# Layer 1's values in couples: seven block products beside keys and queries, values kept in DRAM

## The chip, the core and the metric

The kernel runs on one core of a Trainium2 chip. Everything is float32. The metric is the device time of one execution in microseconds (us); a measurement is the median of several runs.

A core has five engines that run their own queues in order: PE (matrix products; weights are loaded by an instruction of their own, PEld), DVE (elementwise and reductions), ACT (copies and functions such as the exponential), POOL (used here for a few additions) and SP, which here only issues DMAs. Products land in banks of PSUM, 128 partitions by 512 numbers; ACT or DVE take them from there to SBUF. DRAM is reached by DMA alone.

## The reference

Two layers on an input of 2 batches, 512 channels and 64x32 = 2048 tokens. The change touches the second one's attention, a Nystrom attention with 8 heads of 64 and 256 landmarks.

```python
# layer 0: softmax attention over 2048 tokens, with a residual; then
def _L1_attn_ref(x, Wqkv, Wout, bout, conv_w):        # x: layer-normalised tokens
    qkv = x @ Wqkv
    q, k, v = jnp.split(qkv, 3, axis=-1)
    q, k, v = (tohead(q), tohead(k), tohead(v))
    q = q * scale
    qL = q.reshape(b, h, m, l, d).sum(axis=3) / l     # landmarks: means of l = 8 tokens
    kL = k.reshape(b, h, m, l, d).sum(axis=3) / l
    attn1 = softmax(einsum('bhid,bhjd->bhij', q, kL))
    attn2 = softmax(einsum('bhid,bhjd->bhij', qL, kL))
    attn3 = softmax(einsum('bhid,bhjd->bhij', qL, k))
    attn2_pinv = moore_penrose_iter_pinv(attn2, 6)    # six iterations of 256x256 products
    out = attn1 @ (attn2_pinv @ (attn3 @ v))
    res = conv_general_dilated(v, conv_w, ...)        # 33 taps along the tokens, per head
    return (out + res).transpose(0, 2, 1, 3).reshape(b, n, h * d) @ Wout + bout

t = t + _L1_attn_ref(_ln_t(t), ...)
t = t + _L1_ffn_ref(_ln_t(t), ...)                    # one 512x512 map
```

## The kernel before

Heads go in pairs: a pair is 2 heads, 128 columns of a weight. There are 4 pairs in each of 2 batches. Tokens go in 4 blocks (`TB` = 512), the 512 channels in 4 chunks of 128 (`KC`). A 1 MB tile holds 128 rows by 2048 tokens, or 512 channels by 512 tokens.

The order of work on PE, DVE, ACT and POOL is the order in which the program is written: generators yield after a few instructions, and others are advanced between. DMAs on SP may be placed earlier than they are written, when what they wait for is done.

**Keys and queries of layer 1** (`Unit`, `products`, `others`; about 1366 to 1653 us). For a pair, the key and query weights (512x256) against two blocks of tokens (512x1024) are two by two blocks, and seven products of blocks replace eight (Winograd's form of Strassen's scheme). Sums of weights come from `Pair.combine_w` (4 additions on DVE), differences of tokens from `Combined.sums` (4 for each half of the tokens, made once for all pairs). A unit is one pair with one half of the tokens. Its products 1, 6, 7 and 4 are chained: they accumulate in one bank, which ACT copies out after each; products 2, 5 and 3 go to two other banks and are added to the copies by DVE. In the order of issue products 4 and 3 of a unit stand inside the next one: 1, 4 of the last, 2, 3 of the last, 6, 5, 7. `between` and `meanwhile` start loads of the next pair's weights, and attention 2 of the pair before: scores and exponentials (`attend`), then the Gram matrix (`gram`). `later` and `last_of_all` are lists of small DVE calls (landmark sums, largest entries for a bounds check); `some()` makes one of them. `stored` sends finished keys and queries to DRAM. Pair 0 of the first batch is done earlier, beside layer 0's attention; `ORDER` weaves the others of that batch with the rest of layer 0.

**Values** (`values`, `values_of_tokens`, L1148 to L1160). A pair's values are computed with a weight of their own (`prefetch_w`) by plain products: for each block of tokens 4 parts by 4 chunks, each 128x128 by 128 columns; ACT copies the bank out. The result stays in SBUF. The first pair's values stand in the products' stage (`START`), the second's before the iterations, the others' among the last steps of the pair two places earlier (`vals`). For the first batch's pairs, which come second, the tokens are loaded again (`xh2`).

**The iterations** (`pinv`, from 1672 us, one pair after the other: the second batch's pairs, then the first's). Five iterations, each with the squares `pa` and `pb` for two heads, then the last steps: three rounds of a product `wp`, its copy by ACT, transposes `tp`, and a subtraction by DVE, each needing the one before. `chunk(c)` puts other work behind iteration c: for c = 0 to 3 a part of attention 3 of the next pair (`sc<-L,k`, `av<-p,v`) and a block of attention 1 of the pair before (`sc<-q,L`, `av<-p,u`, row sums `rs`, and 1/sums, which eight DMAs from `spread` copy over partitions, `rinv`); for c = 4 the row sums of attention 3 and the convolution of the next pair, four banks in one go (`convolution`, L1781). `last(i)` with i = 0 to 5 puts work between the last steps: values, the next pair's landmark work (`landmarks_values`, `start_values`), and the next attention's first scores. `n_ones` is the number of blocks of attention 1 in the chunks: four, in the last two pairs three and the fourth in `last`. From the fifth pair on, `TURNS` says where units of the second batch's finish (`f`: output projection, norm, map) are made; `o` are units of its last block made early. `TAIL` orders what is left after the last pair. Convolutions wait in SBUF; two of them (`o_d`) in DRAM. Keys and values share a ring of two 1 MB buffers (tag "v").

Of the kernel before, what the change touches and what calls it, by code (L numbers as in the profile page):

```python
# [16 lines left out]
P = 128  # L17
B, C, H, W = 2, 512, 64, 32
S = H * W
# [18 lines left out]
def general_path(  # L38
# [623 lines left out]
TURNS = (  # L662
    (",,,", "f,,,", "f,,,", "f,,,", "f,", "f,f,f,f,f,"),
    ("f,,,", "ff,,,", "f,,,", "f,,,", "f,", "f,f,f,f,f,f"),
    ("fff,,,", "ff,,,", "f,,,", "f,,,", "ff,", ",f,f,f,f,"),
    ("fffoo,,,", "f,f,f,", "f,f,f,", "ff,,oo,", "f,", ",f,,f,f,ff"),
)

TAIL = "11fffnf11f1ff1afafff1f1f1f1faas11bsbs11bbt"
# [4 lines left out]
START = "v....v...,a,v,,,0,1,v".split(",")  # L674

PREFETCH = 26
# [12 lines left out]
def fast_path(  # L689
# [54 lines left out]
    k_d = dram.tile([B, NPAIR, P, S], F32, name="k_fd")  # L744
    X_d = dram.tile([B, NPAIR, 2, P, 2, LM], F32, name="X_fd")
# [728 lines left out]
    class Pair:  # L1474
# [14 lines left out]
        def begin(self, *kinds):  # L1489
            self.w = getattr(self, "w", {})  # L1490
            for j in kinds or (1, 0):
                self.w[j] = self.load_w(j)

        def keys_and_queries(self, pool, tag, xhs, k=None):

            self.begin_landmarks(NTB)
            if k is None:
                k = kvpool.tile([P, S], F32, tag="k", name=f"k_{self.name}")
            q = pool.tile([P, S], F32, tag=tag, name=f"q_{self.name}")
            for t in range(NTB):  # L1500
                toks = slice(t * TB, (t + 1) * TB)
                for j, dst in ((1, k), (0, q)):
                    pp = bank(f"pp{j}_{self.name}_{t}")
                    for c in range(KC):
                        nc.tensor.matmul(
                            pp, lhsT=self.w[j][:, c, :], rhs=xhs[t][:, c, :], start=c == 0, stop=c == KC - 1
                        )
                    nc.scalar.copy(dst[:, toks], pp)
                    for call in self.stored(j, t, dst[:, toks], toks):
                        call()  # L1510
                    yield
            self.bounds()
# [74 lines left out]
        def two(self, kind, name):  # L1587

            name = f"{name}_{self.i}"
            if self.b == 0 and self.hp + 1 < NPAIR:  # L1590
                p = ppool.tile([P, 4 * (LM + 1)], F32, tag="p", name=name)
                p = p.rearrange("p (h k n) -> p h k n", h=2, k=2)
                return [p[:, h] for h in range(2)]
            return [zpool.tile([P, 2, LM + 1], F32, tag=f"{kind}{h}", name=f"{name}_{h}") for h in range(2)]
# [66 lines left out]
        def prefetch_w(self, w=None):  # L1661
            self.w2 = self.load_w(2, w)

        def prefetch(self):
# [3 lines left out]
            nc.sync.dma_start(self.L[0], L_d[self.b, self.hp][:, 0, :])  # L1668
            self.band = lmpool.tile([P, 2, BAND], F32, tag="band", name=f"band_{self.name}", bufs=1)
# [3 lines left out]

        def values(self, xhs):
            v = kvpool.tile([P, NST, P], F32, tag="v", name=f"v_{self.name}")
            self.v = v
            for t in range(NTB):
                values_of_tokens(v, t, xhs[t], lambda k: self.w2[:, k, :], self.name)
                yield
# [101 lines left out]
        def convolution(self, o):  # L1781

            self.o = o
            for t in range(NTB):
# [22 lines left out]
                if t % 2:  # L1807
                    yield
# [147 lines left out]
        def attn1_end(self, t):  # L1956

            rinv, toks = self.rinv1, slice(t * TB, (t + 1) * TB)
            nc.vector.tensor_tensor(rinv, self.av1[t], rinv, ALU.mult)  # L1959
            nc.gpsimd.tensor_tensor(self.o[:, toks], self.o[:, toks], rinv, ALU.add)  # L1960

# [226 lines left out]
    class Unit:  # L2188

        def __init__(self, pair, tp, part):
            self.pair, self.tp, self.part = pair, tp, part
            self.name = f"{pair.name}_{tp}"

        def begin(self, banks_of):
            if self.pair.b == 0 and (self.pair.hp, self.tp) in ((2, 0), (3, 1)):
                d = kvpool.tile([P, NST, P], F32, tag="v", name=f"kq_{self.name}").rearrange("p a b -> p (a b)")
            else:
                d = kvpool.tile([P, S], F32, tag="k", name=f"kq_{self.name}")  # L2200
# [3 lines left out]
        def product(self, to, m, start=True):  # L2204
            w, x = self.pair.ws[m], self.part.of[m]
            for k in range(2):
                nc.tensor.matmul(  # L2207
                    to, lhsT=w[:, k, :], rhs=x[:, k, :], start=start and k == 0, stop=k == 1, skip_group_check=True
                )
# [35 lines left out]
    def products(units, banks_of, between, meanwhile):  # L2245
# [25 lines left out]
        for n, u in enumerate(units):  # L2271
            if n > 2 - u.pair.b:
                until(lambda: not units[n - 3 + u.pair.b].left)
            if u.tp == 0:
                u.pair.begin_landmarks(2)
            u.begin(banks_of)
# [28 lines left out]
        yield  # L2305
        third(last)
        yield

    def others(b, first, parts, banks_of, after=lambda tp: None):

        units = [Unit(pair, tp, part) for pair in pairs[b][first:] for tp, part in enumerate(parts)]
        fronts = {}

        def begin(hp):
            pairs[b][hp].begin()
            fronts[hp] = pairs[b][hp].combine_w()

        def meanwhile(u, m):

            hp = u.pair.hp  # L2320
            if m == 2 and u.tp == 1 and hp:
                before = pairs[b][hp - 1]
                until(lambda: all(before.marked))
                later[:0] = before.attend()
                yield
            if m == 7 and u.tp == 1 and hp:
                until(lambda: pairs[b][hp - 1].attended)
                for h in range(2):
                    pairs[b][hp - 1].gram(h)
                    yield  # L2330

        def between(u, m):
            hp = u.pair.hp
            if m == 2 and u.tp == 1:
                if hp + 1 < NPAIR:
                    begin(hp + 1)
                elif b + 1 < B:
                    pairs[b + 1][0].begin()
            if m == 7 and u.tp == 1 and hp + 1 < NPAIR:
                later.extend(fronts[hp + 1][:3])  # L2340
            if m == 3 and hp + 1 == NPAIR and u.tp == 1:
                after(0)
            if m == 3 and u.tp == 0 and hp > first:
                later.append(fronts[hp][3])

        yield from products(units, banks_of, between, meanwhile)
# [5 lines left out]
    def load_next(tp):  # L2352
        assert over
        next_xhs.extend(load_x(xh_d, 1, "xh", 2 * tp, 2))
# [14 lines left out]
    pairs[0][1].begin()  # L2369
    later.extend(pairs[0][1].combine_w())  # L2370
    later.extend(parts[1].sums())
    more = [others(0, 1, parts, banks_first, load_next)]
# [48 lines left out]
    over = True  # L2421
    while more:
# [8 lines left out]
    xhs = next_xhs  # L2431
    def beside_second(x1lo):
        flat = [qopool.tile([P, S], F32, tag="qo", name=f"t{j}_second") for j in range(2)]
        return [t[:, lo : lo + 2 * TB].rearrange("p (k n) -> p k n", k=2) for t in flat for lo in (0, 2 * TB)]

    parts = [Combined(*xhs[2 * tp : 2 * tp + 2], beside_second) for tp in range(2)]
    todo = pairs[1] + pairs[0]

    def values(n):

        yield from todo[n].values(xhs_of[n // NPAIR])
        if n == NPAIR - 1:
            xhs_of.append(load_x(xh_d, 0, "xh2"))

    def convolution(n):

        name = f"o_{todo[n].name}"
        if n <= NPAIR:
            o = qopool.tile([P, S], F32, tag="qo", name=name)
        else:  # L2450
            o = None if n < len(todo) - 1 else late_buffer(name)
        return todo[n].convolution(o)

    def second_of_first():
# [3 lines left out]
        for part in (landmarks, conv, landmarks, start, conv):  # L2458
# [9 lines left out]


    xhs_of = [xhs]  # L2470
    todo[0].prefetch_w(block_of(lpool, "xr", "w2_first")[:, :, :P])
    later.extend(parts[0].sums())
    later.extend(todo[0].combine_w())
    later.extend(parts[1].sums())
    firsts = [values(0)]

    def beside(events):
        for c in events:
            if c == "v":
                advance(firsts)  # L2480
            elif c == "a":
                until(lambda: all(pairs[0][-1].marked))
                later[:0] = pairs[0][-1].attend()
            elif c in "01":
                until(lambda: pairs[0][-1].attended)
                pairs[0][-1].gram(int(c))
            else:
                some()

    beside(START[0])  # L2490
    first = second_of_first()
    for i, _ in enumerate(others(1, 0, parts, banks_second)):
# [6 lines left out]
        if i + 1 < len(START):  # L2499
            beside(START[i + 1])  # L2500
        if i == PREFETCH:
            todo[0].prefetch()
        if i >= PREFETCH + 6 and i % 2:
            next(first, None)
    for _ in first:
        some(2)
    todo[1].prefetch_w()


# [4 lines left out]
    vals = [values(1)]  # L2514
    advance(vals)
    until(lambda: all(todo[NPAIR - 1].marked))
    later[:0] = todo[NPAIR - 1].attend()
    advance(vals)
# [291 lines left out]
```

## Time and profile before

| what | us |
|---|---|
| median of 3 runs (2649.33 to 2650.98) | 2649.54 |
| the profiled execution | 2649.55 |
| its span | 2647.7 |
| PE busy in 0 to 1240 (layer 0, mostly) | 1233.08 of 1240.00 |
| PE busy in 1240 to 1366 | 125.55 of 126.00 |
| PE busy in 1672 to 1755 (the first pair's iterations) | 83.00 of 83.00 |
| PE busy in 1851 to 2377 (pairs three to seven) | 523.92 of 526.00 |
| PE busy in 2474 to 2647 (the tail) | 164.02 of 173.00 |

The span is what the profiler saw of the program. A group's row of the page holds line, engine, operation, written<-read tiles, shapes and count, then busy time, mean of one in ns, and the engine's idle time ahead of them with what ended it. A row of the timeline holds start, length, engine, line, operation and tiles; a row of waits between brackets names the instruction that ended the wait. A matmul's length includes its way through the array, so rows overlap: what one costs is read from start to start.

### The profile page before, as it was taken

To read this page: it belongs to the slowest core of one execution; us is meant where nothing else is said; L and a number is where in the kernel's file an instruction comes from. 1 tells how busy PE (TensorE), PEld (TensorE's weight loads), DVE (VectorE), ACT (ScalarE), POOL (GpSimd) and SP (SyncE) were. 2 spreads that over 40 slices of the span, in tenths; PEclk is the share of its full clock that TensorE was granted. 3 is DMA by queue.
4 is the path that set the end of the run, shared out by engine and by line. 5 is a ranking of instruction groups with operands and counts; after the bars stand their busy time and mean duration, and the time that the engine had idled before them with its cause. 6 is when DMAs were issued, how large, how long until landed. Compare 5 with 4: busy or idle time off the path is not lost.

```text
span 2647.7 us, 41440 instructions
## 1 busy us (share of the span) xinstructions
PE 2623.1 (99%) x16882; PEld 1353.3 (51%) x16882; DVE 1780.1 (67%) x2259; ACT 921.0 (35%) x1398; POOL 169.6 (6%) x127
## 2 busy tenths in 40 slices
PE   9999999999999999999999999999999999999998
PEld 5343443444344344353344555777677666665444
DVE  5788897886667778767867866544644645465665
ACT  1444453443344434435522323223333232231310
POOL 0011011000001100000002000000000000000000
PEclk9999999999999999999999999999999999999999
DMA  4011011201221201011115633213111112121211
GB/s 147 22 30 36 13 33 49 77 21 52 88 80 58 91 25 32 25 56 60 41 44 182 225 125 118 98 33 129 48 37 61 60 45 100 34 81 36 97 35 49
DMA packets 123608, 177.16 MB, mean 67 GB/s; under 512 B 16784, under 2 KB 77968, under 8 KB 120848
## 3 DMA queue, kind: packets, MB, share of 16 engines
q1 hardware_dynamic: 117264, 153.15, 17.8%
q0 software_dynamic: 5440, 20.97, 2.0%
q8 instruction: 134, 2.20, 0.4%
q14 instruction: 66, 0.54, 0.1%
q10 hardware_dynamic: 704, 0.31, 0.0%
HBM read 94.02 MB, written 63.57 MB: 60 GB/s over the span
## 4 chain that ended last, share of the span: by engine, by line
PE 91%; DVE 6%; issue 1%; ACT 1%; DMA 1%; SPq 0%; DVEq 0%; ACTq 0%
PE av_f L1319 15%; PE sc_f L1289 15%; PE pb L1866 5%; PE pa L1866 5%; PE vp_f L1153 4%; PE yp_g L1168 4%; PE yp_f L1168 4%; PE fp_g L2022 4%; PE vp L1153 4%; PE pc_f L1021 3%; PE pu L2207 3%; DVE acc_f L1307 3%; PE pu_f L1021 2%; PE sc L1695 2%; PE sc L1923 2%; PE av L1716 2%
## 5 line engine op out<-in xcount | busy, mean ns | idle before, releaser
L1297 ACT ACTIVATE p_f<-sc_f 128x1024 f32<-128x1024 f32 x512 | 496.5, 1021 | 540.2 <-PE sc_f L1289 540.0
L1307 DVE TENSOR_TENSOR acc_f<-acc_f,p_f 128x1024 f32<-128x1024 f32 x448 | 575.3, 1284 | 110.8 <-ACT p_f L1297 83.9
L1319 PE MATMUL av_f<-p_f,v_f 64*64 64x512 f32 x4096 | 494.4, 589 | 2.8 <-DVE q_f L1326 2.8
L1289 PE MATMUL sc_f<-q_f,k_f 64*64 64x512 f32 x4096 | 489.9, 591 | 0.3 <-ACT p_f L1297 0.3
L1319 PEld LDWEIGHTS av_f<-p_f,v_f 64*64 64x64 f32 x4096 | 162.5, 133 | 286.8 <-issue 274.3
L1289 PEld LDWEIGHTS sc_f<-q_f,k_f 64*64 64x64 f32 x4096 | 154.2, 133 | 282.2 <-issue 277.2
L1866 PE MATMUL pa<-M 128*128 128x192 f32 (+1 forms) x640 | 150.3, 380 | 0.0
L1866 PE MATMUL pb<-R 128*128 128x192 f32 (+1 forms) x640 | 149.3, 380 | 0.6 <-DVE M L1879 0.6
L1153 PEld LDWEIGHTS vp_f<-wv_f,x 128*128 128x128 f32 x1024 | 115.8, 192 | 5.5 <-issue 5.2
L1866 PEld LDWEIGHTS pb<-R 128*128 128x128 f32 x640 | 106.5, 190 | 23.6 <-DVE M L1879 0.8
L1866 PEld LDWEIGHTS pa<-M 128*128 128x128 f32 x640 | 108.2, 193 | 19.8 <-ACT M L1857 2.0
L1153 PE MATMUL vp_f<-wv_f,x 128*128 128x128 f32 x1024 | 117.9, 276 | 0.0
L1168 PE MATMUL yp_g<-o,wo_f 128*128 128x512 f32 x256 | 113.8, 595 | 0.0
L1168 PE MATMUL yp_f<-q_f,wo_f 128*128 128x512 f32 x256 | 112.4, 595 | 0.1
L1339 POOL TENSOR_TENSOR q_f<-q_f,rinv_f 128x512 f32<-128x512 f32 x32 | 49.0, 1530 | 970.1 <-DMA rinv_f<-acc_f 647.5
L1153 PE MATMUL vp<-w,xh 128*128 128x128 f32 x896 | 105.8, 276 | 0.0
L1153 PEld LDWEIGHTS vp<-w,xh 128*128 128x128 f32 x896 | 102.2, 192 | 5.4 <-issue 3.5
L1879 DVE SCALAR_TENSOR_TENSOR M<-M,pb 128x320 f32<-128x320 f32 (+1 forms) x160 | 60.1, 417 | 60.8 <-PE pb L1866 60.8
L2022 PE MATMUL fp_g<-xn_g,mT 128*128 128x512 f32 (+1 forms) x232 | 99.3, 579 | 0.0
L1928 ACT ACTIVATE p<-sc 128x512 f32<-128x512 f32 x128 | 66.7, 602 | 91.6 <-PE sc L1923 91.1
L1960 POOL TENSOR_TENSOR o<-o,rinv 128x512 f32<-128x512 f32 x32 | 44.4, 1386 | 772.9 <-DVE rinv L1959 587.5
L1879 DVE SCALAR_TENSOR_TENSOR R<-M,pa 128x320 f32<-128x320 f32 (+1 forms) x160 | 58.5, 407 | 42.1 <-PE pa L1866 42.1
(293 smaller groups left out, 3215.9 us busy)
## 6 DMA issues: line engine op xcount, KB each, us to landing
xh<-xh_fd SPq DMA_DIRECT2D x12, 1024.0 KB, 7.9
rinv_f<-acc_f SPq DMA_DIRECT2D x256, 32.0 KB, 1.9
xr_f<-in_x_dram SPq DMA_DIRECT2D x8, 1024.0 KB, 5.2
x_fd<-xr_f POOLq DMA_DIRECT2D x8, 1024.0 KB, 4.7
xh_fd<-xn_f POOLq DMA_DIRECT2D x8, 1024.0 KB, 4.4
k_fd<-kq SPq DMA_DIRECT2D x16, 512.0 KB, 2.6
q_fd<-kq SPq DMA_DIRECT2D x16, 512.0 KB, 3.2
k<-k_fd SPq DMA_DIRECT2D x8, 1024.0 KB, 6.0
```

Of the source, the lines that this page charges most:

```text
L1021: nc.tensor.matmul(to, lhsT=w[:, k, :], rhs=x[:, k, :], start=start and k == 0, stop=k == 1, skip_group_check=True,)
L1153: nc.tensor.matmul(vp[:, j * P : (j + 1) * P], lhsT=xb[:, k, j * P : (j + 1) * P], rhs=w_of(k), start=k == 0, stop=k == KC - 1,)
L1168: nc.tensor.matmul(yp, lhsT=wo_sb[:, k, m * P : (m + 1) * P], rhs=oTs[k][:, toks], start=k == 0, stop=k == NPAIR - 1,)
L1289: nc.tensor.matmul(sc[r * D : (r + 1) * D, h, :], lhsT=hd.k[rows, lo : lo + D], rhs=hd.q[rows, t * TB : (t + 1) * TB], start=True, stop=True,)
L1297: nc.scalar.activation(p, sc, AF.Exp, scale=D**-0.5)
L1307: nc.vector.tensor_tensor(acc, first if c == 1 else acc, p, ALU.add)
L1319: nc.tensor.matmul(av[r][half, :], lhsT=hd.v[keys, c, half], rhs=pp[keys, h, :], start=c == 0, stop=c == NST - 1,)
L1866: nc.tensor.matmul(dst, lhsT=lhsT[:, k, t * P : (t + 1) * P], rhs=rhs[:, k, :], start=k == 0, stop=k == 1)
L1879: nc.vector.scalar_tensor_tensor(out, m, scale, pr, ALU.mult, ALU.subtract)
L1928: nc.scalar.activation(p[:, h, :], sc, AF.Exp, scale=D**-0.5)
L2022: nc.tensor.matmul(fp[:, cols], lhsT=mT[:, k, m * P : (m + 1) * P], rhs=self.xn[:, k, cols], start=k == 0, stop=k == KC - 1,)
L2207: nc.tensor.matmul(to, lhsT=w[:, k, :], rhs=x[:, k, :], start=start and k == 0, stop=k == 1, skip_group_check=True)
```

## The change

The values of two pairs of one batch become a `Couple`, which stands in the products' stage like a pair: its two weights take the place of key and query weights, and its two halves of tokens are two `Unit`s of seven products. As values are needed with tokens on partitions, tokens are now the left operand: `operands` splits a product of 512 columns into four parts of 128 columns. `ITEMS` gives the order for a batch (4 and 5 are the couples of pairs 0, 1 and 2, 3). Values go to DRAM (`v_d`) and come back by `prefetch_v`, a pair ahead; keys come by `prefetch_k` from the last steps of the pair before that. The plain products of layer 1's values, their weights' loads, the second load of the first batch's tokens and the way of two convolutions through DRAM go.

The convolution yields after each block, and `LAST` puts its four portions (c), the rest of the landmark work (l) and the start values (s) between the last steps. Attention 1 has three blocks in the chunks and the fourth in the last steps for every pair that has one before it. The first batch's four couple-halves run after `ORDER` is through; the second batch's tokens are loaded in two steps, the first already there. With the second batch's last couple stand attention 2 of its last pair and the start of the iterations (`at_end`); in the table `at`, True stands for the scores of the pair before and False for its Gram products, and a pair gives its unit and product. `TURNS`, `OUTS` and `TAIL` place units of the finish anew.

```diff
+TURNS = "000020000200110001001111|300010000000111020100020|310010001000100000221110|310020002000200010011222"
+OUTS = "000001000000001001000000"
+LAST = "c|lc|s|c|cs|"
+ITEMS = "12345", "041235"
-TAIL = "11fffnf11f1ff1afafff1f1f1f1faas11bsbs11bbt"
+TAIL = "11fffnf11f1ff1afafff1f1faf11fas11bsbs11bbt"
-START = "v....v...,a,v,,,0,1,v".split(",")
-PREFETCH = 26
+PREFETCH = 36
...
+    v_d = dram.tile([B, NPAIR, P, S], F32, name="v_fd")
...
+        def operands(self, w, x):
+            return [(slice(0, TB), [(w[:, k, :], x[:, k, :]) for k in range(2)])]
...
-        def prefetch(self):
+        def prefetch_k(self):
             self.k = kvpool.tile([P, S], F32, tag="v", name=f"k2_{self.name}")
             nc.sync.dma_start(self.k, k_d[self.b, self.hp])
...
+        def prefetch_v(self):
+            self.v = kvpool.tile([P, NST, P], F32, tag="v", name=f"v_{self.name}")
+            nc.sync.dma_start(self.v, v_d[self.b, self.hp].rearrange("p (c d) -> p c d", d=P))
...
-                if t % 2:
-                    yield
+                yield
...
+    class Couple(Pair):
+        def begin(self):
+            self.w = {1 - j: pairs[self.b][self.hp + j].load_w(2) for j in range(2)}
+
+        def operands(self, w, x):
+            parts = [slice(j * P, (j + 1) * P) for j in range(TB // P)]
+            return [(part, [(x[:, k, part], w[:, k, :]) for k in range(2)]) for part in parts]
...
+        def stored(self, j, part, tokens, toks):
+            nc.sync.dma_start(v_d[self.b, self.hp + 1 - j][:, toks], tokens)
+            return [lambda: None]
...
         def product(self, to, m, start=True):
-            w, x = self.pair.ws[m], self.part.of[m]
-            for k in range(2):
-                nc.tensor.matmul(
-                    to, lhsT=w[:, k, :], rhs=x[:, k, :], start=start and k == 0, stop=k == 1, skip_group_check=True
-                )
+            for n, (cols, operands) in enumerate(self.pair.operands(self.pair.ws[m], self.part.of[m])):
+                for k, (left, right) in enumerate(operands):
+                    nc.tensor.matmul(
+                        to[:, cols], lhsT=left, rhs=right,
+                        start=start and n + k == 0, stop=k == 1, skip_group_check=True,
+                    )
...
         fourth(last)
         yield
+        at_end()
         third(last)
...
+                first, second = ((0, 7), (1, 2)) if early and n + 1 == len(items) else ((1, 2), (1, 7))
+                at[item, first] = prev, True
+                at[item, second] = prev, False
...
     def load_next(tp):
         assert over
-        next_xhs.extend(load_x(xh_d, 1, "xh", 2 * tp, 2))
+        if tp:
+            return
+        next_xhs.extend(load_x(xh_d, 1, "xh", 2, 2))
...
     over = True
+    for t, tag in enumerate(("xr", "xn")):
+        next_xhs.append(block_of(lpool, tag, f"xh_1_{t}"))
+        nc.sync.dma_start(next_xhs[t], chunked(xh_d[1])[:, :, t * TB : (t + 1) * TB])
     while more:
         advance(more)
...
-        while vals:
-            advance(vals)
         if after:
-            after.prefetch()
+            after.prefetch_v()
             after.attn3_begin()
-        if n + 2 < len(todo):
-            vals = [values(n + 2)]
...
         def chunk(c):
+            if c == 0 and n > 1:
+                todo[n - 2].attn1_end(n_ones)
...
-                    drain(convolution(n + 1))
+                    conv = convolution(n + 1)
...
-                kinds = (product_bank, bank) if c and before else (bank, product_bank)
+                kinds = (product_bank, bank) if c and ones_before else (bank, product_bank)
...
         def last(i):
-            if i == 1 and after:
-                next(landmarks)
-                drain(landmarks)
-                start = after.start_values()
-            if i == 2 and after:
-                next(start)
-            else:
-                advance(vals)
-            if i == 3 and after:
-                next(start)
-            if n_ones < NTB:
+            for part in LAST.split("|")[i] if after else "":
+                if part == "l":
+                    drain(landmarks)
+                    start = after.start_values()
+                else:
+                    next({"c": conv, "s": start}[part])
+            if i == 0 and n + 2 < len(todo):
+                todo[n + 2].prefetch_k()
+            if before:
                 if i == 0:
                     before.attn1_scores(n_ones, 0)
                     before.attn1_scores(n_ones, 1)
                     before.attn1_add(n_ones)
...
-        n_ones = NTB if n + 2 < len(todo) else NTB - 1
+        n_ones = NTB - 1
```

## The prediction

> **What bounds the kernel now.** I read the busy times and the chain that ended last, then the stretches, then PE's order of time in the stages that the change touches.
>
> ```profile
> span 2647.7 us, 41440 instructions
> PE 2623.1 (99%) x16882; PEld 1353.3 (51%) x16882; DVE 1780.1 (67%) x2259; ACT 921.0 (35%) x1398; POOL 169.6 (6%) x127
> PE 91%; DVE 6%; issue 1%; ACT 1%; DMA 1%; SPq 0%; DVEq 0%; ACTq 0%
> L1153 PE MATMUL vp<-w,xh 128*128 128x128 f32 x896 | 105.8, 276 | 0.0
> ```
>
> PE is 91% of the last chain, so what PE issues is what the kernel costs, as long as its cover holds. The last row is layer 1's values: it never waits (0.0). With the 128 of the first pair these are 1024 instructions (8 pairs x 4 blocks of tokens x 4 parts x 4 chunks, and each matmul of this type is two instructions: 32 in the rows below for 16 in the code).
>
> ```profile
> 1366.00:1500.00 134.00, 131.19 (x346) 60.52 (x344) 106.18 (x134) 38.76 (x60) 19.34 (x14) 1.00 0.55 193
> 1500.00:1653.00 153.00, 152.84 (x683) 84.48 (x684) 100.26 (x170) 42.19 (x84) 0.00 (x0) 1.00 0.36 123
> 1653.00:1672.00 19.00, 18.80 (x151) 17.38 (x150) 15.00 (x37) 4.13 (x9) 0.37 (x1) 1.00 0.84 295
> 1755.00:1851.00 96.00, 96.00 (x676) 68.39 (x672) 50.71 (x96) 30.39 (x75) 5.94 (x4) 1.00 0.25 84
> 2377.00:2474.00 97.00, 94.69 (x385) 51.85 (x384) 54.31 (x99) 21.51 (x52) 5.26 (x6) 1.00 0.24 81
> ```
>
> Columns: stretch, length, busy PE, PEld, DVE, ACT, POOL, PE's clock, DMA share, GB/s. The first two are layer 1's products for keys and queries, the third the values left before the iterations, the fourth the second pair's iterations, the fifth the last pair's. PE is full everywhere but in the last pair. Busy PE is modelled, so I went to starts. The second pair's last steps (us from start, us):
>
> ```profile
> 1822.79 1.08 PE L1740 MATMUL rs<-acc,ones 128*64 128x256 f32 x8
> 1823.70 5.00 PE L1793 MATMUL cv<-band,v 128*64 128x144 f32 x88
> 1829.01 1.37 PE L1841 MATMUL wp<-M 128*64 128x256 f32 x8
> 1830.31 3.84 PE L1153 MATMUL vp<-w,xh 128*128 128x128 f32 x32
> 1833.98 0.38 PE L1850 MATMUL tp<-ident,R 128*128 128x128 f32 x2
> 1834.42 3.74 PE L1153 MATMUL vp<-w,xh 128*128 128x128 f32 x32
> 1838.09 1.08 PE L1841 MATMUL wp<-M,R 128*64 128x256 f32 x8
> ```
>
> Each row starts as the one before ends (1834.42 to 1838.09 is 3.67): values and the convolution are the cover of the serial chain wp, copy, tp, subtraction. The question is what this chain does with less cover.
>
> **The parts.** (1) Values by seven products. 896 instructions of the same shape (4 couples x 2 halves of the tokens x 7 products x 16) take the place of 1024. A run of 64 goes from 1500.16 to 1507.38: 112.8 ns each. 32 runs of 3.64 (between 3.57 and 3.67) are 116.5 us. In the products stage runs of one shape follow each other without a cut (1540.75 to 1542.46 is one product), so I take 3.57/32 = 111.6 ns there: 896 x 111.6 = 100.0 us. **-16.5**; at 112.8 on both sides it is -14.4.
> [...]
>
> (2) Its side work. ACT copies: four for each half of a couple, 32 in all as before. DVE: 3 additions x 8 halves x 0.69 (row of kq<-pb,kq: 685 ns) = 16.5 us, and 16 sums of weights x 0.42 = 6.7. They come with 100 us of PE work and without the two 1.21 us reductions that every piece of a key or query needs, in stages where DVE is busy 79% and 66%. Token combinations are those of keys and queries, kept. Nothing on the path: **0**; without the cover at most a bank's addition per product, 0.69 x 24 = 16.5.
>
> (3) DRAM. 16 stores of 512 KB and 8 loads of 1 MB come; the 4 loads of layer 1's input for the second batch (7.9 us to landing), 8 stores of 256 KB and 2 loads of 1 MB of convolutions go. Ten issues more on SP, about 0.4 us each. SP is where it could hurt: the load of a pair's values stands behind the eight issues of the last 1/sums, which now come at the end of every pair. In the last pair but one they are:
>
> ```profile
> 2368.20 4.95 SPq L816 DMA_DIRECT2D rinv<-acc  x8
> k<-k_fd SPq DMA_DIRECT2D x8, 1024.0 KB, 6.0
> q<-q_fd SPq DMA_DIRECT2D x7, 1024.0 KB, 4.8
> ```
>
> Counting from a pair's first product, the issues end about +2 and the values land at +8. They are wanted after two rounds of pa and pb (7.4), the scores (1.82) and the other pair's values (1.77): +11.0; 3 us spare. **0**; if the cover goes, see the slow rival. For the first pair both loads can go while the products still run, since their buffers are free once its own attention and convolution are done.
>
> (4) Convolution in four portions. One run of 88: 1823.70 to 1828.64, 4.94. Two halves in the products stage: 2.52 and 2.57, 5.09. A cut costs 0.15. Seven pairs x 3 cuts and the first pair's 2: 23 x 0.15 = **+3.5** (0 if a cut falls where another run was cut anyway).
>
> (5) The fourth ones-block of attention 1 (scores 1.82, values 1.77, sums 0.57) moves from the fourth iteration to the last steps in pairs 2 to 6. It costs there what it cost before. The iteration it leaves looks like those of the first pair: scores and values of attention 3 from 1679.88 to 1684.17, 4.29, against 1.82 + 1.83 beside the other work: +0.64 x 5 = 3.2. In pair 7 these had the wrong order of banks and took 4.79 (2334.22 to 2339.01); the edit of `kinds` gives back 0.5. **+2.7** (0 to 3.2).
>
> (6) Last steps with less cover. Four value runs of 3.6 us go. The last pair shows what thin cover costs:
>
> ```profile
> 2459.03 0.33 PE L1856 MATMUL tp_M<-ident,M 128*128 128x128 f32 x1 [0.47 <-DVE M L1879]
> 2465.08 1.27 PE L1841 MATMUL wp<-M,R 128*64 128x256 f32 x8 [0.39 <-DVE R L1879]
> 2467.69 1.28 PE L1841 MATMUL wp<-M,R 128*64 128x256 f32 x8 [0.38 <-DVE R L1879]
> ```
>
> 1.24 us a pair, with nothing but attention 1 between. Behind tp_M come the row sums (0.91), behind the other two a convolution portion (1.2), each longer than these waits. ACT must get through the copy of wp (0.37), the portion's copy (0.59) and four exponentials (2.06) before DVE can add (1.28) and subtract (0.48): 4.8 us after wp, while PE has 1.25 + 1.82 + 0.44 + 1.25 + 1.77 = 6.5 to do. I take 0.2 a pair for seven pairs, **+1.4**, between 0 and 8.7.
>
> (7) Ends. The change of batch had 2.73 for a product of 1.72 (1497.43 to 1500.16), waiting for the second batch; its first halves are now loaded some 48 turns earlier: -1.0. The last couple forces DVE's marks of the pair before, and only three products (5.4 us) stand between its scores and its Gram products, whose chain on DVE took 4.5 us (1660.63 to 1665.1): +1.0. In the last pair eight units of the finish stand in the last steps, five before: most of the 1.24 goes, **-1.0**, and the tail has five fewer left, **+0.5** (-3 to +3 for both).
>
> Sum: -16.5 + 3.5 + 2.7 + 1.4 - 0.5 = **-9.4**. The profiled execution took 2649.55 (span and 1.85 around it), 0.01 from the median: 2649.55 - 9.4 = 2640.1, **2640 us**. With each part at its ends: -16.5 - 1 - 3 = -20 (2629), and -14.4 + 3.5 + 3.2 + 8.7 + 3 = +4 (2653).
>
> **Rivals.** *A larger gain.* Cuts and the lighter iteration cost nothing, because the number of runs in the last steps hardly changes: -16.5 - 1.0 - 2 = 2630. For it: value runs were cut too. Against: 4.29 in the first pair.
> *The last steps become latency bound.* Every pair waits as the last one does, 7 x 1.24 = 8.7, in place of 1.4: 2647, no change. Against: the portion behind each wait is longer than the wait.
> *Slower: values land late.* PE is in order, so attention 3's values stand in front of the whole iteration. If the load goes out behind the 1 MB of queries as well, it lands at +2.4 + 10.8 (the slowest q) = +13.2, 2.2 late, and a blocked SP delays the 1/sums too: about 2.2 in 7 pairs, 15.4, and it decides from 9.4/7 = 1.3 us a pair: 2655. For it: more work on SP at just this place. Against: SP issues when buffers are free, ahead of need elsewhere.
> [...]
> *Not what it says.* The 128-column products might be bound by weight loads (186 to 192 ns): 896 x 0.19 = 170 us, 2705. The same loads run at 112.8 a piece in the values of before, so hardly.
>
> **Chances.** Forecast 0.68, larger gain 0.14, latency bound 0.10, late values 0.06, weight loads 0.02. The likeliest alone: 2633 to 2646 (parts 4 to 7 at half their ends). Range **2630 to 2648**: it takes in the third case and half of the second, and leaves out the slow ones. A measurement here tells 0.2%, 5.3 us, from no change. Faster: 0.68 x 0.93 + 0.14 + 0.02 = **0.79**; same: 0.05 + 0.08 = **0.13**; slower **0.08**.
>
> **What would show it.** Groups of Unit's product with 128 columns, 896 in all, about 112 ns from start to start, and no values at L1153's helper after layer 0; pairs 1 to 6 some 14 us shorter each, the products stage some 70 us longer than before with the values of two pairs taken off it; cv in runs of 22 in the last steps; waits of PE for DVE R and M under 0.3 a pair. Wrong: idle PE before av<-p,v put down to a DMA of v; tp or wp rows with waits near 0.4; products that wait for ACT or DVE; a tail longer than 173 us.

## The result

The changed kernel took 2640.80 us (median of 7 runs, 2639.60 to 2641.22), the kernel before 2649.54 (2649.33 to 2650.98). The ratio is 0.9964, its 95% interval 0.9954 to 0.9973: 8.7 us less, faster by more than 0.2%. The forecast was 2640.

The page of the kernel after, its first lines, the chain that ended last, one row of DMA issues; and of the groups of instructions two that hold products of the couples:

```profile
span 2638.8 us, 41283 instructions
...
PE 2613.0 (99%) x16754; PEld 1345.5 (51%) x16754; DVE 1805.8 (68%) x2299; ACT 921.6 (35%) x1398; POOL 175.7 (7%) x127
...
PE 92%; DVE 5%; ACT 1%; issue 1%; DMA 1%; DVEq 0%; SPq 0%; ACTq 0%
...
v_fd<-kq_v SPq DMA_DIRECT2D x16, 512.0 KB, 3.1
...
L2203 PE MATMUL pu_v<-w,xh 128*128 128x128 f32 x192 | 23.2, 276 | 0.0
...
L2203 PE MATMUL pu_v<-w,t_second 128*128 128x128 f32 x128 | 15.7, 276 | 0.7 <-ACT kq_v L2210 0.7
```

PE has 16754 matmuls where it had 16882: the 128 that seven products save against eight. Stretches of after (columns as in the prediction): most of the products, the second pair's iterations, and the last pair's last steps with the start of the tail.

```profile
1526.00:1727.00 201.00, 199.50 (x1099) 130.39 (x1098) 108.35 (x174) 49.55 (x95) 0.00 (x0) 1.00 0.41 143
...
1815.30:1880.00 64.70, 64.70 (x381) 43.75 (x380) 41.48 (x76) 19.42 (x50) 4.66 (x3) 1.00 0.16 52
...
2440.00:2500.00 60.00, 54.63 (x183) 22.00 (x182) 32.74 (x38) 16.39 (x30) 4.25 (x2) 0.94 0.30 101
```

PE is still full in the iterations. The products' row lacks 1.5 us, waits of 0.68 and 0.83 that come up below. The last row has 5.4 us of idle time and a clock of 0.94. Where the 8.9 us of the span came from is told by the starts of each pair's first `p_pa` in the timelines:

| stretch | before, us | after, us | difference |
|---|---|---|---|
| span's start to the first product of the stage | 1245.03 | 1245.45 | +0.42 |
| products, to the first pair's iterations | 427.41 | 501.25 | +73.84 |
| pair 1 | 83.01 | 68.63 | -14.38 |
| pairs 2, 3, 4, each | 95.59 | 81.95 | -13.64 |
| pair 5 | 111.65 | 97.60 | -14.05 |
| pair 6 | 116.57 | 108.55 | -8.02 |
| pair 7 | 106.84 | 102.40 | -4.44 |
| last pair and tail, to the last matmul's start | 261.89 | 262.59 | +0.70 |
| behind it | 8.5 | 6.5 | -2.0 |

The values left the six pairs' last steps (24 runs of some 3.65 us, 87.6). The products' stage grew by 74 us: it gained the products of all eight pairs and lost the plain values of two that stood there (29.2). The difference of the two is 13.8; waits and seams in the iterations and the last pair took 4.9 of it back.

### The profile page after: what moved, and what is told of

It reads as the page before. It is cut to its first block, busy times and chain, and to the rows that moved or that the text cites. A ratio compares the mean times of both kernels' runs of the same rounds, so it can differ in the third digit from the quotient of the medians.

```text
span 2638.8 us, 41283 instructions
## 1 busy us (share of the span) xinstructions
PE 2613.0 (99%) x16754; PEld 1345.5 (51%) x16754; DVE 1805.8 (68%) x2299; ACT 921.6 (35%) x1398; POOL 175.7 (7%) x127
## 4 chain that ended last, share of the span: by engine, by line
PE 92%; DVE 5%; ACT 1%; issue 1%; DMA 1%; DVEq 0%; SPq 0%; ACTq 0%
PE sc_f L1289 15%; PE av_f L1319 15%; PE pb L1841 5%; PE pa L1841 5%; PE vp_f L1153 4%; PE yp_f L1168 4%; PE fp_g L2020 4%; PE yp_g L1168 4%; PE pc_f L1021 3%; PE pu L2203 3%; DVE acc_f L1307 3%; PE pu_f L1021 2%; PE av L1692 2%; PE sc L1671 2%; PE pu_v L2203 2%; PE av L1914 2%
## 5 line engine op out<-in xcount | busy, mean ns | idle before, releaser
L1903 ACT ACTIVATE p<-sc 128x512 f32<-128x512 f32 x128 | 66.4, 603 | 78.8 <-PE sc L1898 78.3
L1680 ACT ACTIVATE p<-sc 128x512 f32<-128x512 f32 x128 | 66.9, 618 | 60.1 <-PE sc L1671 59.9
L2210 ACT COPY kq<-pu 128x512 f32<-128x512 f32 x56 | 32.5, 586 | 151.4 <-PE pu L2203 134.1
```

Source lines behind the costliest of these rows:

```text
L1680: nc.scalar.activation(p[:, h, :], scs[h], AF.Exp)
```

## The experiments

Each kernel is the one after with the edit shown, timed against the kernel before on the same chip (2650.3 to 2650.8 there).

### An eighth product

```diff
             u.product(u.c, 2)
+            if isinstance(u.pair, Couple):
+                u.product(u.c, 2)
```

> Every half of a couple issues its second product twice, so that the values cost eight products of blocks again, in the changed kernel's schedule; the result is the same. If the gain comes from the products that PE no longer issues, each of the 8 halves pays 1.785 us (16 instructions of 111.6 ns) and the kernel takes 2640.8 + 14.3 = 2655 us: above the kernel before, since the costs of the new schedule then stand alone. If the gain came from the new schedule (the retuned turns, the loads that start earlier) and PE has air in the products' stage, the time stays within 2 us of 2640.8.

2655.70 us (2654.13 to 2656.66), ratio 1.0019 (1.0010 to 1.0029): 14.9 more than after, for 128 instructions, with the pairs as long as they were (68.64, 81.94). The products' stage took 515.55 in place of 501.25, 14.3 more or 112 ns an instruction: a product costs PE its instructions and nothing hides any of it; with eight products the change would have been a loss of 5 us. The whole gain hangs on the product left out.

### The convolution in one go

```diff
-LAST = "c|lc|s|c|cs|"
+LAST = "|l|s||s|"
...
-                    conv = convolution(n + 1)
+                    drain(convolution(n + 1))
```

> The convolution of the next pair goes back behind the fifth iteration in one go of four banks; the last steps of seven pairs keep only landmark work, attention 1 and the finish. If the portions are what covers the chain of wp, copy, transposes and subtraction, the waits appear: in the first pair after each wp (copy, about 0.6 us) and after each tp (subtraction, about 0.6 us), some 3 us in that pair and 1 to 2 us in the next three, less where units of the finish stand; against it the cuts come back, 0.2 us a pair. Together 4 to 8 us longer, 2645 to 2649. If attention 1 and the landmark work are cover enough, the time falls by the cuts alone, 1 to 2 us, to about 2639.

2651.72 us (2650.74 to 2653.94), ratio 1.0005 (0.9996 to 1.0015): 10.9 more than after, beyond the 4 to 8 that were expected. The pairs grew by 1.95, 1.66 (three times), 2.2, 0.9 and 1.3 us. The timeline of PE in its second pair's last steps (start, length in us):

```profile
1882.17 5.00 PE L1769 MATMUL cv<-band,v 128*64 128x144 f32 x88
1887.10 0.44 PE L1831 MATMUL tp_M<-ident,M 128*128 128x128 f32 x2
...
1896.14 0.44 PE L1825 MATMUL tp<-ident,R 128*128 128x128 f32 x2
1896.96 1.27 PE L1816 MATMUL wp<-M,R 128*64 128x256 f32 x8 [0.38 <-DVE R L1854]
1898.16 0.44 PE L1825 MATMUL tp_y<-ident,wide 128*128 128x128 f32 x2
```

The same place in the kernel after:

```profile
1880.01 0.44 PE L1831 MATMUL tp_M<-ident,M 128*128 128x128 f32 x2
...
1890.82 0.44 PE L1825 MATMUL tp<-ident,R 128*128 128x128 f32 x2
1891.19 1.45 PE L1769 MATMUL cv<-band,v 128*64 128x16 f32 x24
1892.47 1.06 PE L1816 MATMUL wp<-M,R 128*64 128x256 f32 x8
1893.37 1.32 PE L1769 MATMUL cv<-band,v 128*64 128x16 f32 x20
```

With a portion behind it a `tp` costs 0.37 from start to start, without one 0.82 (1896.14 to 1896.96, 0.38 of it the wait for DVE's subtraction); `wp` 0.90 against 1.20. From `tp_M` to the next pair the one kernel takes 13.94 with no convolution, the other 17.27 with 5.12 of it, 12.15 beside it: in this pair cover is worth 1.8 us. The cuts cost 0.2 (5.12 in portions, 4.93 in one go).

### The fourth ones-block back in its iteration

```diff
-        n_ones = NTB - 1
+        n_ones = NTB if n + 2 < len(todo) else NTB - 1
```

(and the matching conditions in `chunk` and `last`)

> Pairs two to six make the fourth block of attention 1 in the fourth iteration's chunk again, as before the change; the last steps keep their convolution portions. The changed kernel pays 4.29 us for the scores and values of attention 3 that stand alone there, against 3.65 beside the block: 0.64 in five pairs. If the portions cover the last steps alone, as they seem to do in the first pair, which has no block there, this gives back 3.2 us: 2637.6. If the block was needed as cover in the last steps, waits appear there and the time stays at 2640.8 or rises by up to 1.2 a pair.

2640.85 us (2640.27 to 2641.77), ratio 0.9964 (0.9950 to 0.9977): no change against after, a miss. The stages of pairs 2 and 4 became 0.65 shorter (81.27 and 81.33), but that of pair 3 took 82.54, and 5 and 6 grew by 0.55 and 0.74. The wait in pair 3, in the timelines of PE, DVE and SP's queue:

```profile
1968.82 0.44 PE L1735 MATMUL tp<-ident,acc 128*128 128x128 f32 x2 [1.34 <-DVE acc L1727]
```

```profile
1965.89 0.69 DVE L1934 TENSOR_TENSOR rinv<-av,rinv 128x512 f32<-128x512 f32 x1 [1.59 <-DMA rinv<-acc]
1966.49 1.74 DVE L1726 RECIPROCAL acc<-acc 128x256 f32<-128x256 f32 x1
1968.34 0.42 DVE L1727 TENSOR_TENSOR acc<-av,acc 128x256 f32<-128x256 f32 x1
```

```profile
1958.29 5.89 SPq L816 DMA_DIRECT2D rinv<-acc  x8
```

DVE took this work in the order of the program: the block's multiplication by 1/sum waits 1.59 us for its DMAs, and the landmarks' reciprocal, which needs none of that, starts behind it at 1966.49; PE then waits 1.34 for the landmarks. In pair 2 the same eight issues took 4.95 us in place of 5.89, the multiplication waited 0.31, and nothing was late. A test of this reading comes last. Pairs 5 and 6 had little to win: units of the finish stand between the scores and the values of their lighter iteration, and these take 3.81 (1.93 and 1.88) in the kernel after, not 4.29. In pair 5 PE now waits 0.15 and 0.33 for DVE in the last steps. In pair 6 the scores of the two attentions take 4.59 side by side (2223.40 to 2227.99) where pair 5 has 3.69, as they did in pair 6 before the change; why is open.

### The finish later

The last six digits of `TURNS` place the units of the finish in the last pair's last steps; four of the eight go to the tail.

```diff
-... 310020002000200010011222"
+... 310020002000200010011110"
```

> Four of the eight units of the finish in the last pair's last steps go to the tail (the last six digits of the turns become 011110). In the changed kernel PE waits some 9 us between 2472 and 2491 us for the early block's normalisation, with too little else left. If those waits are the price of the units moved out of the tail, most of it comes back: 5 to 8 us shorter, 2633 to 2636, while each of the last steps still has 3.4 us of cover. If the waits only move to another place, or the last steps miss their cover (1.2 us), the time stays within 2 us of 2640.8.

2633.90 us (2633.74 to 2634.64), ratio 0.9938 (0.9924 to 0.9952). The last pair and the tail take 255.66 in place of 262.59, and no other stretch moved. The tail's start in the kernel after:

```profile
2477.76 0.64 PE L805 MATMUL rs<-acc,ones 128*32 128x256 f32 x8 [1.28 <-DVE acc L1907]
...
2482.82 1.12 PE L1898 MATMUL sc<-q,L 64*128 64x512 f32 x2 [1.46 <-DVE xn_g_early L1191]
2486.57 2.05 PE L1206 MATMUL var_g<-sq_g,mean_w 128*128 128x512 f32 x2 [2.63 <-DVE sq_g L1203]
2488.55 3.15 PE L1914 MATMUL av<-p,u 128*64 128x512 f32 x8
```

and with the finish later:

```profile
2470.85 3.70 PE L2020 MATMUL fp_g<-xn_g,mT 128*128 128x512 f32 x8
2474.39 3.60 PE L1168 MATMUL yp_g<-o,wo_f 128*128 128x512 f32 x8
2477.91 2.04 PE L1898 MATMUL sc<-q,L 64*128 64x512 f32 x8
2480.91 1.10 PE L1190 MATMUL mean_g<-xn_g_early,mean_w 128*128 128x512 f32 x2 [0.95 <-DVE xn_g_early L1187]
2481.93 1.94 PE L1914 MATMUL av<-p,u 128*64 128x512 f32 x8
```

After the change the norm of the early block (`xn_g_early`, `sq_g`) meets the attention's sums with too little other work for PE: three waits, 5.4 us together (not the 9 of the expectation). With the units kept for this place, of which `fp_g` and `yp_g` show on PE, one wait of 0.95 is left. That is 4.4 of the 6.9 us; the slow `av<-p,u` (3.15 for 1.94) stands where the granted clock read 0.50, of which the last section tells.

### The values' load, two and four times

```diff
+            for _ in range(2):
-            nc.sync.dma_start(self.v, ...)
+                nc.sync.dma_start(self.v, ...)
```

> The load of the values' halves from DRAM is issued twice over, to the same tile, so that the values land later. In the changed kernel the load of a pair lands some 6.2 us after the pair's first product and its first reader, the first fused block, starts at 11.35: 5.2 us to spare. Theory (the values are ahead by that spare): a second load of 512 KB costs 3.3 to 5.4 us, which the spare just holds; the time stays within 2 us of 2641. Rival (values land just in time, each microsecond later is a microsecond on the path): 7 x 3.3 to 5.4 = 23 to 38 us longer, 2664 to 2679.

> The same load is issued four times over. It should land 10 to 16 us later, that is 16 to 22 us after the pair's first product, and the first fused block is wanted at 11.35. Theory (5.2 us spare, and past it every microsecond counts): a wait of 5 to 11 us ahead of the first fused block in six or seven pairs, 25 to 70 us longer: 2666 to 2711. If other work ahead of that block on TensorE still covers it, nothing changes.

One run each: 2641.16 and 2698.17 us. (The transfer is 1 MB, as its row of issues has it, not the 512 KB of the expectation, whose 3.3 to 5.4 us were the author's estimate; in the kernel after these loads took 4.8 to 6.8 to landing.) SP's queue and PE in the kernel after, third pair, whose first product starts at 1897.28:

```profile
1894.69 3.76 SPq L816 DMA_DIRECT2D rinv<-acc  x6
1898.55 0.53 SPq L1651 DMA_DIRECT2D v<-v_fd  x1
```

```profile
1908.63 1.90 PE L1692 MATMUL av<-p,v 128*64 128x256 f32 x16
```

Issued at +1.27 and some 4.9 us to landing (the median), +6.2; read at +11.35. With the load twice over, the second one is issued at 1904.58, and PE waits 0.30 us for it in this pair; the pairs grow by at most 0.52. With four:

```profile
1922.09 1.94 PE L1915 MATMUL av<-p,u 128*64 128x512 f32 x8
1933.95 3.54 PE L1693 MATMUL av<-p,v 128*64 128x256 f32 x16 [9.92 <-DMA v<-v_fd]
```

The five pairs from 2 to 6 take 9.0, 11.7, 12.1, 11.4 and 6.3 us more, the seventh none, and the first starts 6.2 later. So the values were ahead by some 5 us, and past that each microsecond counts on the path (the third pair waits 9.92 and grows by 11.7; after the wait its 16 products take 3.54 in place of 1.90, at a granted clock of 0.50 up to 1937): the slow rival's mechanism is real, and its condition was not met.

### The second half's values an iteration later

```diff
             if after and ones_before:
                 after.attn3_values(2 * c + 1)
+            elif after:
+                kept.append(2 * c + 1)
```

on top of the finish later; `kept` is made between the next iteration's scores.

> On top of finish_later (2633.9): in the iterations without an attention 1 block the second half's product with the values is kept until after the next iteration's first scores, so that TensorE has work while ScalarE makes the exponentials. Theory (the light iteration's 4.29 us against 3.65 of work is a wait of the second half's product for its exponentials): some 0.5 us in each of 10 iterations (four in the first pair, one in each of six others), less 4 to 5 us: 2629 to 2630. Rival (the wait goes elsewhere, to VectorE or ScalarE in the next iteration): 2633 to 2635.

2633.11 us (2632.87 to 2634.56), ratio 0.9934 (0.9921 to 0.9948), against 0.9938 without it: no gain. A light iteration of the first pair with the finish later alone (`sc` to `p_pa` is 4.30):

```profile
1766.23 2.00 PE L1671 MATMUL sc<-L,k 64*128 64x256 f32 x16
1768.16 2.43 PE L1692 MATMUL av<-p,v 128*64 128x256 f32 x16
1770.53 0.33 PE L1831 MATMUL p_pa<-ident,M 128*128 128x128 f32 x1
```

and with the values kept:

```profile
1765.75 1.14 PE L1671 MATMUL sc<-L,k 64*128 64x256 f32 x8
1766.81 1.08 PE L1692 MATMUL av<-p,v 128*64 128x256 f32 x8
1767.83 1.13 PE L1671 MATMUL sc<-L,k 64*128 64x256 f32 x8
1768.89 1.08 PE L1692 MATMUL av<-p,v 128*64 128x256 f32 x8
1769.91 0.33 PE L1831 MATMUL p_pa<-ident,M 128*128 128x128 f32 x1
```

4.16: four runs of 8 at 1.02 to 1.06 take the place of two runs of 16 that are 1.82 each beside other work. Each change of kind costs about 0.1 (1.04 against 0.91), and the seams take back most of what the wait gave. In the second pair PE then waits 0.19 for DVE's `M` in place of the exponentials.

### A portion between product 7 and product 4

The last couple's products 7 and 4 follow each other on one bank, and the second waits for ACT to copy the first. The last convolution portion of the first pair is kept for this place.

```diff
+        while held:
+            drain(held.pop())
         fourth(last)
```

> On top of lag_late: the last portion of the first pair's convolution is kept back and put between product 7 and product 4 of the last couple's half, where product 4 waits 0.97 us for the marks of product 7's bank. Theory: that wait is covered by 1.2 us of convolution, less 0.9 us: 0.9 under lag_late. Rival (the wait moves on to the next product of that bank or to the last steps of the first pair, which lose that portion): no gain, or 0.5 longer.

> finish_later with the last convolution portion of the first pair kept for the place between product 7 and product 4 of the last couple's half, without the change of lag_late. Theory (the wait of 0.68 us there is covered, and the first pair starts about 1 us earlier; lag_late gave nothing): 1 us under finish_later's 2633.9, 2632.5 to 2633.5. Rival (lag_late's 0.5 us in the first pair counts): 2633.5 or more.

2632.11 us (2631.92 to 2635.30), ratio 0.9934 (0.9921 to 0.9948), and 2633.61 (2632.31 to 2634.29), ratio 0.9933 (0.9920 to 0.9947): each some 1 us or less under the kernel without it (2633.11 and 2633.90), with runs that overlap: the times alone can't tell a difference. The place itself, in the kernel with the finish later and then with the portion kept (without the values an iteration later):

```profile
1740.56 1.95 PE L2203 MATMUL pu_v<-w,t_second 128*128 128x128 f32 x16
1743.18 2.05 PE L2203 MATMUL pu_v<-w,t_second 128*128 128x128 f32 x16 [0.68 <-ACT kq_v L2210]
```

```profile
1739.89 1.95 PE L2203 MATMUL pu_v<-w,t_second 128*128 128x128 f32 x16
1741.77 1.37 PE L1769 MATMUL cv<-band,v 128*64 128x16 f32 x20
1743.08 2.05 PE L2203 MATMUL pu_v<-w,t_second 128*128 128x128 f32 x16
```

The wait is gone. From the first product of the values to the first pair's iterations it is 249.56 us in place of 250.56, 1.0 as expected, and the same two numbers stand in the two kernels with the values an iteration later. But the stretch from the first product of a key to that point was 0.6 longer in this execution, and the program's first scores came at 53.63 in place of 53.38: what lies ahead of this place differs between executions by nearly as much as the gain. The gain is shown at its place, not in the whole time.

### The fourth block back, its end behind the landmarks

```diff
-        n_ones = NTB - 1
+        n_ones = NTB if n < NPAIR else NTB - 1
...
+            if before and n_ones == NTB and i == 2:
+                before.attn1_end(NTB - 1)
```

> On top of late_held: the fourth ones-block is back in the fourth iteration in the stages of pairs 2 to 4 alone, and its end (the multiplication by 1/sum, which waits for its DMA) is moved from the last iteration to the last steps, behind VectorE's work for the landmarks. Theory (in fourth_block_in_chunk pair 3 lost its 0.64 since the end stood on VectorE ahead of the landmarks' reciprocal and waited 1.59 us for the DMA): 0.6 us shorter in each of the three pairs, 1.9 less than late_held, near 2631. Rival (the loss in pair 3 had another cause): pairs 2 and 4 shorter by 0.6 and pair 3 not, 1.3 less or under.

2630.63 us (2629.82 to 2631.00), ratio 0.9923 (0.9909 to 0.9936), 3.0 under the kernel without it on the same chip, whose runs lie all above. The stages of pairs 2, 3 and 4 take 81.05, 81.08 and 81.06 in place of 81.95: pair 3 gains as the others do. DVE in the third pair's stage:

```profile
1963.74 1.75 DVE L1726 RECIPROCAL acc<-acc 128x256 f32<-128x256 f32 x1 [0.70 <-ACT acc L1725]
...
1966.66 0.69 DVE L1934 TENSOR_TENSOR rinv<-av,rinv 128x512 f32<-128x512 f32 x1
```

The multiplication by 1/sum now comes behind the landmarks and finds its DMAs done, though the eight issues took 5.94 us in this pair. The gain is 0.9 a pair, not 0.64: the iterations grow by 3.52 and the last steps shrink by 4.41, for a block of 4.16. With issues as slow as before pair 3 no longer loses its 0.6, so the order on DVE was the cause. This is the fastest kernel of the study, 10 us under after.

## Why the prediction was right

By its own terms, from start to start:

| step | predicted | measured | from |
|---|---|---|---|
| 1 values by seven products | -16.5 | -16.0 | 56 runs at 1.785 and eight seams of 0.1, 100.8, against 32 runs at 3.65, 116.8 |
| 2 side work: product 4 waits for product 7's bank | 0 | +1.9 | twice 0.94: product 7 takes 2.62 and product 4 1.89, for 1.785 each |
| 3 DRAM | 0 | 0 | no PE wait put down to it |
| 4 convolution in portions | +3.5 | +1.6 | 0.2 in each of seven pairs, 0.2 for the first pair's in the products' stage |
| 5 lighter iterations | +2.7 | +0.7 | +0.64 in each of pairs 2 to 4 (4.29), +0.1 in 5, -0.8 in 6, -0.5 in 7 (4.29 for 4.79) |
| 6 last steps with less cover | +1.4 | about +0.6 | left over in pairs 1 to 5: some 0.1 each in 2 to 4, 0.2 in 5 |
| 7 ends | -0.5 | +1.8 | pairs 6, 7, the last and what lies behind it: -13.75, less the terms above |
| left over in the products' stage | | +0.1 | |
| sum | -9.4 | -9.3 | and +0.4, the start of the stage |

The mechanism was the one that was forecast: fewer products on a full PE, at a price of some 7 us for seams, waits and cover. That the sum meets the measured value within 0.1 is luck: the terms of steps 1, 2 and 7 came out 4.7 worse than forecast, those of 4, 5 and 6 4.7 better. Rows 6 and 7 are remainders, so the measured column adds up by its making.

**Step 1** carried it, and the eighth product confirms its price. The rival of weight loads is out: a load takes 186 to 192 ns in the couples' products too, and their instructions follow each other at 111.6.

**Step 2** put the side work at nothing, and one piece of it stands on the path: in the last half of each batch's last couple, product 4 comes right behind 7, and ACT must copy the bank out between (PE waits 0.68 for it). Before the change Gram products stood there.

**Step 3** had the right order and too little margin: the load goes out at +1.27, not +2, and was ahead by 5 us, not 3. The 1/sums do stand just ahead of it on SP. The four loads show that the rival's mechanism would have cost what it said, about a microsecond for each that the values are late. (The four loads of the input that go are the second load of the first batch's tokens, not the second batch's.)

**Step 4 and step 6** belong together, and there the sizes were off. In the last steps cuts cost 0.07 each (0.2 for three), not 0.15, and they bought cover: without the portions the second pair's last steps have 1.8 us more, above the 1.24 by which the latency-bound rival was priced. That rival's mechanism is real, and what the prediction said against it, the portion behind each wait, is what kept it away: with the convolution in one go the change would have gained nothing (ratio 1.0005).

**Step 5** had the right price, 0.64, but in three pairs, not five. In pairs 5 and 6 units of the finish fill the lighter iteration, and it costs 0.1; pair 6 gains 0.9 besides, since its two score runs, which took 4.59 side by side before (2211.96 to 2216.55), now stand apart. What it costs is a wait only in part; the values an iteration later show that seams make up the rest. That the block's end then lies on DVE ahead of the landmarks wasn't in the prediction, and it decides whether the block can go back.

**Step 7** was wrong in its terms. The change of batch kept the microsecond that was to go: it stands now behind the last product of the values,

```profile
1552.93 1.95 PE L2203 MATMUL pb_v<-s_v,xh 128*128 128x128 f32 x16
1555.71 1.96 PE L2203 MATMUL pu<-xh,w 128*128 128x512 f32 x4 [0.83 <-issue]
```

in the timeline of PE after. The second batch's first tokens were loaded by then (the two loads went out at 1439.55 and 1459.32 and took at most 10.5 us), so the wait is not for them, as the prediction had it. The profile names no instruction that ended it, and its cause stays open. The marks and the last Gram products cost nothing new: the wait at the landmarks' scores (`sc<-L,L`) is 1.60 from start to start as it was 1.59. The eight finish units in the last pair's last steps did fill them, but in the tail they were missing: 5.4 us of waits, where the term allowed at most 3. Units that left the last pair's iterations (75.0 us from its start to `tp_M`, 81.0 before) made up for most of it. The finish later shows that 7 us lay there.

## What to carry to other kernels

A product saved on a full TensorE was worth its instructions here (112 ns each) and no more, so ask first what the removed work covered and give the serial chain other cover, in portions, at the places of its waits; cuts are cheap (0.07 us here) beside a wait. On an engine that works in order, as DVE did here (its wait of 1.59 us for DMAs was followed by one of 1.34 on PE), keep an operation that waits for a DMA behind those that the path needs next; moved by a few instructions, the same block turned in pair 3 from a loss of 0.6 us to a gain of 0.9. When work is moved, look again at the list of what fills the end: a hand-written order is right only for the kernel that it was written for.

## What the runs showed of the hardware

In the tail of the kernel after the granted clock fell to 0.50, and the longest wait ahead of the fall, from 2440 on, was 1.46. Stretches there (us; the columns as before, the clock third from the end):

```profile
2481.00:2482.80 1.80, 0.36 (x1) 0.00 (x0) 1.76 (x1) 0.00 (x1) 0.00 (x0) 1.00 0.76 279
2482.80:2484.00 1.20, 1.12 (x2) 0.29 (x2) 0.00 (x0) 1.20 (x2) 0.00 (x0) 1.00 0.22 63
2484.00:2485.00 1.00, 0.00 (x0) 0.00 (x0) 0.59 (x1) 1.00 (x3) 0.00 (x0) 0.61 0.13 36
...
2490.00:2491.00 1.00, 1.00 (x4) 0.24 (x2) 1.00 (x1) 0.00 (x0) 0.00 (x0) 0.50 0.10 20
2491.00:2492.00 1.00, 1.00 (x5) 0.30 (x2) 1.00 (x1) 0.00 (x0) 0.00 (x0) 0.98 0.00 0
```

It fell within 2484 to 2485 (0.61 over that microsecond), when TensorE had been idle for less than 1 us, after a wait of 1.46 and 1.1 us of work. It read 0.50 from 2485 to 2491 and 0.98 in the microsecond after that, 4.4 us after the work resumed at 2486.57. Until then `var_g` took 1.98 from start to start and `av<-p,u` 3.08; with the finish later, at a clock of 1.00 from 2440 to 2500 and with one wait of 0.95 left, 0.86 and 1.87: some 2.3 of the 6.9 us that the finish later gained. Over the whole span the runs of after and those of the eighth product, the convolution in one go, the fourth block in its iteration and the load twice over have a mean clock of 0.998 or 0.999, those of the five kernels built on the finish later 0.999 or 1.000. With four loads it is 0.990: around the wait of 9.92 in the third pair (1924.03 to 1933.95) the clock read 1.00 in 1924 to 1926, 0.74 in the next 2 us, 0.50 from 1928 to 1937 and 0.89 in the microsecond after, and 16 products with the values took 3.54 for 1.90. What sets off a fall, these runs don't show.
